# Third layer's first two blocks: corners weighted and summed inside the attention instead of after it, with the second layer's remaining work spread anew

## The chip, the cores and the metric

The kernel runs on one core of one Trainium2 chip. A core has TensorE (PE, matrix multiplies), VectorE (DVE), ScalarE (ACT), GpSimd (POOL), SyncE (SP, which issues DMAs), and 16 DMA engines. Each engine works through its own queue of instructions in order. The metric is the device time of one execution in microseconds (us), as the median of several runs.

## The reference, cut to what matters

Four layers follow each other on an image batch x of shape (2, 256, 64, 64), all in float32.

- Layer 0: a group norm, then self-attention with 4 heads of 64 channels over the 4096 pixels of each image, a projection, and a residual.
- Layer 1: a position term is added.
- Layer 2 (the "second layer" of the code): a bottleneck. A 1x1 convolution to 64 channels, a modulated deformable 3x3 convolution, a 1x1 convolution back to 256 channels, and a residual.
- Layer 3 (the "third layer"): group norm, ReLU, deformable 3x3 convolution, and that once more, with a residual.

A deformable convolution samples the image, for each pixel and each of nine taps, at a computed place between pixels. The sample is a weighted sum of four corners:

```python
out = gather(y0, x0) * (wy0 * wx0) + gather(y0, x0 + 1) * (wy0 * wx1) \
    + gather(y0 + 1, x0) * (wy1 * wx0) + gather(y0 + 1, x0 + 1) * (wy1 * wx1)
off = conv(conv(x, dw, groups=C), pw)          # where to sample
res = einsum('bckhw,ock->bohw', sampled, w)    # nine taps, 256 channels in, 256 out
```

## The kernel before

**Two phases.** `attention` holds layer 0 and 1 and, in the gaps, most of layer 2 and the very beginning of layer 3. `deform` holds the rest of layer 2 and layer 3. The order of instructions on PE, ACT, DVE and POOL is the order in which the Python program emits them.

**Attention.** The loop variable n runs over 1024 tiles of scores (4 units of 256; a block is 16 tiles) and advances by 2, so an *iteration* is two tiles. For each tile PE makes scores (L580), DVE takes their maximum (L592), ACT takes exponentials (L598), PE transposes them (`turn`, L610), DVE and ACT copy the transposes out of PSUM (`keep`, L627 and L629), and PE multiplies them with the values (`attend`, L639). Exponentials are emitted one iteration ahead of their transposes. Once per block, POOL scales the block's output with shares that SP has written to DRAM and loaded back (`spread`, L506 and L510; `combine`, L519, L520, L525).

**Early samples.** In the last unit `early_samples` computes sampling places for the first two blocks (EARLY = 2) of 512 pixels of layer 3, image 0. Two blocks of 9 taps by 4 groups of 128 pixels are 72 *steps*. For each, the inner function `gather` lets POOL fetch all four corners of 128 pixels (128 rows of 4 KB, L846), and SP stores this raw tile into the DRAM tensor `samp_d` (L1259). `self.sample()` calls it once at the end of each iteration, and twice where n % 16 is 10, 12 or 14.

**Deform.** The loop variable s runs over 1152 steps (4 passes of 8 blocks of 36 steps). `gather(s + 8)` fetches corners (POOL, L846; for the first 72 steps a load from `samp_d`, L1445). `first` multiplies the first corner by its weight on ACT (L1459). `others` adds the other three on DVE, one scalar_tensor_tensor each (L1465). `turn` transposes the sample on PE (L1477), `evacuate` copies it out on ACT (L1486), and `product` multiplies it with the convolution's weights on PE (L1496).

**Side work.** A `Side` emits pieces of another computation between the steps. `second` is the deformable convolution of layer 2 for image 1: 144 conv steps, each with two gathers on POOL (`bfour`, L846), a multiplication (L1065) and two additions (L1075, L1076) on DVE, kept eight tiles deep. It advances by up to 0.9 s + 2.5 min(s, 72) pieces, two pieces a conv step. When it is through, `image` of pass 1 is started, 0.9 pieces a step; whatever is left of it is emitted at s = 228. `offs` holds the sampling places of the next blocks (its matmuls are L803 and L823).

```python
seconds = Side(0, 0.9, second, lambda s: 2.5 * min(s, EARLY * BLOCK))
...
images.append(Side(s, 0.9, image(*layers[1])))
```

Of the kernel before, what the change touches and what calls it, by code (L numbers as in the profile page):

```python
# [64 lines left out]
class Net:  # L65
    def __init__(self, ctx, tc, a, out):
        self.tc, self.nc, self.a, self.out = tc, tc.nc, a, out
        nc = self.nc
        const = ctx.enter_context(tc.tile_pool(name="const", bufs=1))
        self.small = ctx.enter_context(tc.tile_pool(name="small", bufs=2))  # L70
        dram = ctx.enter_context(tc.tile_pool(name="dram", bufs=1, space=DRAM))

        self.ident = const.tile([P, P], F32, name="ident")
        make_identity(nc, self.ident)
        self.vec = const.tile([P, V_COLS], F32, name="vec")
        nc.sync.dma_start(self.vec, a["vec"])
        self.sel = const.tile([P, 32], F32, name="sel")
        self.shift = const.tile([P, DWK, 32], F32, name="shift")
        self.later = [(self.sel, a["sel"]), (self.shift, a["shift"])]

        self.img2, self.img3, self.x2d = [], [], []

        self.xn_d, self.xa_d = [], []
        for b in range(B):
            self.img2.append(dram.tile([GH * GW, 2 * CM], F32, name=f"img2_{b}"))
            self.img3.append(dram.tile([GH * GW, 2 * C], F32, name=f"img3_{b}"))
            self.x2d.append(dram.tile([C, HW], F32, name=f"x2d_{b}"))
            self.xn_d.append(dram.tile([C, HW], F32, name=f"xn_{b}"))
            self.xa_d.append(dram.tile([C, HW], F32, name=f"xa_{b}"))

        self.pos_d = dram.tile([C, HW], F32, name="pos_d")

        self.samp_d = [dram.tile([4 * K2 * P, 4 * C], F32, name=f"samp_d{i}") for i in range(EARLY)]
        self.sample = lambda: False
        self.early = {}
        self.share_d = [dram.tile([16, P], F32, name=f"share_d{n}") for n in range(2)]

        vec = self.vec
        self.bn_s = const.tile([P, 4], F32, name="bn_s")
        self.bn_t = const.tile([P, 4], F32, name="bn_t")  # L100
        rstd = self.rsqrt(vec[:, V_BNV : V_BNV + 4], 4)
        nc.vector.tensor_mul(self.bn_s, rstd, vec[:, V_BNG : V_BNG + 4])
        m = self.small.tile([P, 4], F32, name="bn_m")
        nc.vector.tensor_copy(m, vec[:, V_BNM : V_BNM + 4])

        nc.vector.tensor_sub(m[:, 1:2], m[:, 1:2], vec[:, V_DCNB : V_DCNB + 1])
        nc.vector.tensor_mul(m, m, self.bn_s)
        nc.vector.tensor_sub(self.bn_t, vec[:, V_BNB : V_BNB + 4], m)

        for v in (self.bn_s, self.bn_t):  # L110
            nc.vector.tensor_copy(v[CM:P, 0:2], v[0:CM, 0:2])
# [69 lines left out]
    def attention(self, bott):  # L181
# [5 lines left out]
        with ExitStack() as ctx:  # L187
# [489 lines left out]
            while n < last + 4 or back or more or any(own.values()):  # L677
                u, d = divmod(n, per_unit)
                if d == 0 and u < len(units):
                    plan_unit(u)  # L680
                    if u == 0:
                        back.append(prepare(1))
                    if u == 1:
                        back.append(bott.before(0, bt, ps))
                    if u == 2:
                        back.append(first_batch())
                    if u == 3:
                        back.insert(0, bott.before(1, bt, ps))
                        back.append(self.early_samples(bott, bt, held, xp, vp, kp, ps))

                def small(at):
                    steps = own.pop(at, ())
                    for f in steps:
                        f()
                    if not steps and u > 1:
                        background(1)

                if n - 1 in pts:
                    p = pts.pop(n - 1)
                    keep(n - 1, p, "ACT")  # L700
                    keep(n - 1, p, "DVE")
                ps.flush()
                sc = [scores(m) for m in (n + 2, n + 3) if m < last]
                for m in range(len(sc)):
                    lowest(n + 2 + m, sc[m])
                if n < last:
                    p = turn(e.pop(n))
                    keep(n, p, "DVE")
                if sc:
                    e[n + 2] = exponentials(n + 2, sc[0])  # L710
                if n < last:
                    keep(n, p, "ACT")

                small(n)
                if 4 <= n < last + 4:
                    attend(n - 4)
                    attend(n - 3)
                small(n + 1)
                if n < last:
                    pts[n + 1] = turn(e.pop(n + 1))  # L720
                if sc:
                    e[n + 3] = exponentials(n + 3, sc[1])
                if u or n % 8 == 0:
                    background(1)

                for _ in range(1 + (n % 16 in (10, 12, 14))):
                    more = self.sample()
                n += 2
# [486 lines left out]
    def early_samples(self, bott, pools, held, xp, vp, kp, ps):  # L1215
# [33 lines left out]
            self.filters(wf[cb], cb, dw, pw)  # L1249
            yield True  # L1250
        free = deque(x.rearrange("p u n -> p (u n)") for x in xbs)
        gathers, stores = deque(), deque()

        def gather():


            if len(stores) > 1 and len(free) < 3 or not gathers and stores:
                dst, four = stores.popleft()
                nc.sync.dma_start(dst, four)  # L1259
                free.append(four)  # L1260
            if gathers:
                dst, idx = gathers.popleft()
                four = free.popleft()
                self.gather(four, self.img3[0], idx)
                stores.append((dst, four))
            return gathers or stores

        self.sample = gather
        for i in range(EARLY):
            idx = bott.corner.tile([P, 4, K2], I32, name="bidx")  # L1270
            w4 = self.early[i] = bott.corner.tile([P, 4, K2, 4], F32, name="bw4")
            steps = self.offsets(
                i, xs,
                lambda s, row: wf[s][:, DWK * row : DWK * row + DWK, :].rearrange(
# [19 lines left out]
                free.extend(whole)  # L1294
            for m in range(4 * K2):
                k, j = divmod(m, 4)
                gathers.append((self.samp_d[i][m * P : m * P + P, :], idx[:, j, k : k + 1]))

    def deform(self, bott):

# [4 lines left out]
        with ExitStack() as ctx:  # L1305
# [90 lines left out]
                        yield  # L1396

            IMAGE = 4 + 6 * NB + 1
            corners = {(0, 0, i): (None, w4) for i, w4 in self.early.items()}

            def offsets(b, l):
                if b == 0:
# [20 lines left out]
            layers = [(b, l) for l in range(2) for b in range(B)]  # L1423
            BLOCK = 4 * K2
            LAYER, ALL = NB * BLOCK, len(layers) * NB * BLOCK
            AHEAD, LEAD = 8, BLOCK + 16
            due = {}
            fours, smps, pts, sts, outs, ress = {}, {}, {}, {}, {}, {}

# [3 lines left out]
                return n, i, r // 4, r % 4  # L1433

            def gather(s):
                if s < ALL:
                    n, i, k, j = parts(s)
                    b, l = layers[n]
                    fours[s] = gp.tile([P, 4, C], F32, name="four")
                    four = fours[s].rearrange("p s c -> p (s c)")  # L1440
                    if n == 0 and i < EARLY:

                        queue = nc.gpsimd if s < AHEAD else nc.sync
                        m = 4 * k + j
                        queue.dma_start(four, self.samp_d[i][m * P : m * P + P, :])  # L1445
                        return
                    idx = corners[b, l, i][0]
                    self.gather(four, self.img3[b], idx[:, j, k : k + 1])

            def weight(s, c):  # L1450
                n, i, k, j = parts(s)
# [2 lines left out]

            def first(s):

                if s < ALL:
                    smps[s] = sp.tile([P, C], F32, name="smp")
                    nc.scalar.mul(smps[s], fours[s][:, 0], weight(s, 0))  # L1459

            def others(s):
                if s < ALL:
                    four = fours.pop(s)
                    for c in range(1, 4):
                        nc.vector.scalar_tensor_tensor(  # L1465
# [86 lines left out]
            OFFS = 24  # L1552
            inner = ExitStack()
            second = bott.conv(1, bott.pools(inner, 8), ps)
            for s in range(AHEAD):
                gather(s)
                conv_weight(0, s)
            conv_weight(0, AHEAD)
            begun = offsets(0, 0)
            next(begun)  # L1560
            load(0, self.xn_d[0], wp)
            offs = [Side(EARLY * BLOCK - LEAD - 6, OFFS / BLOCK, begun)]
            first(0)


            last = Side(0, 1, bott.last(1, bott.kept, ps))
            seconds = Side(0, 0.9, second, lambda s: 2.5 * min(s, EARLY * BLOCK))
            stats[0] = self.norm_stats()
            images = []
            for s in range(ALL + 12):  # L1570
                n = s // LAYER
                if s == LAYER:
                    stats[1] = self.norm_stats()
                gather(s + AHEAD)
                first(s + 1)
                others(s)
                if (s - 6) % 4 == 0:
                    evacuate((s - 6) // 4)
                product(*divmod(s - 7, 4), s)
                turn(s - 2)  # L1580
                for f in due.pop(s, ()):
                    f()
                last.follow(s)
# [120 lines left out]
```

## Time and profile before

| what | us |
|---|---|
| runs (3) | 5145.72, 5151.03, 5154.88; median 5151.03 |
| span of the profiled execution (the page has no other time for it) | 5149.0 |
| attention, from the span's start to its last products | about 2980 |
| deform, first 72 steps (transposes of step 0 to step 72) | 2997.6 to 3335.2 |
| transposes of step 158 / 228 | 3548.1 / 3664.8 |
| PE / DVE / ACT / POOL busy over the span | 4816.8 / 4196.7 / 2883.6 / 2254.7 |

The page cuts the span into 40 slices of 128.7 us; each digit is the busy share of an engine in tenths. A group line names the line, the engine, the operation and the tiles, then the count, the busy time, the mean in ns, and the idle time before these instructions with what ended it. A window line gives busy times of PE, PE weight loads, DVE, ACT and POOL, then the granted PE clock, the DMA share and GB/s.

### The profile page before, as it was taken

How to read it: one execution, taken by the hardware profiler on the slowest of the kernel's cores; microseconds unless marked ns; L12 is line 12 of the kernel's file. 1: busy time of each engine (PE TensorE's matmuls, PEld its weight loads, DVE VectorE, ACT ScalarE, POOL GpSimd, SP SyncE). 2: the span in 40 equal slices, each digit the busy share in tenths (PEclk: the TensorE clock that was granted, in tenths of full speed). 3: DMA queues.
4: the chain of work that ended last, by engine and by line, in shares of the span. 5: the costliest groups of instructions: out<-in, count | busy, mean ns of one | idle time of the engine just before them, and what ended most of it. 6: DMA issues, size and time to landing. Idle time of an engine off the chain costs nothing. (4 is left out here: it accounts for less than half of the span.)

```text
span 5149.0 us, 100000 instructions
## 1 busy us (share of the span) xinstructions
PE 4816.8 (94%) x38200; PEld 2651.9 (52%) x38200; DVE 4196.7 (82%) x7929; ACT 2883.6 (56%) x5221; POOL 2254.7 (44%) x2256
## 2 busy tenths in 40 slices
PE   8999999999999999999999957679999999999998
PEld 5555565555565555565555523234444444444443
DVE  6878867878668888687766768878999999999998
ACT  5666656666666666666656622235444554454444
POOL 0111111111107777464023257775666566666665
PEclk9999999999999999999999967789999999999999
DMA  5231121111113333322557677679999999999998
GB/s 172 61 99 51 42 68 49 35 46 30 55 52 94 93 100 102 94 85 79 150 193 272 233 242 239 207 251 376 340 329 339 360 359 350 356 388 346 347 348 318
DMA packets 367022, 997.66 MB, mean 194 GB/s; under 512 B 61372, under 2 KB 98810, under 8 KB 366542
## 3 DMA queue, kind: packets, MB, share of 16 engines
q0 software_dynamic: 196560, 690.41, 37.7%
q1 hardware_dynamic: 169438, 300.73, 17.9%
q8 instruction: 300, 4.92, 0.4%
q14 instruction: 180, 1.47, 0.1%
q10 hardware_dynamic: 544, 0.13, 0.0%
HBM read 855.36 MB, written 127.35 MB: 191 GB/s over the span
## 5 line engine op out<-in xcount | busy, mean ns | idle before, releaser
L1465 DVE SCALAR_TENSOR_TENSOR smp<-four,dw,smp 128x256 f32<-128x256 f32 x3240 | 1503.8, 483 | 122.3 <-ACT smp L1459 44.4
L598 ACT ACTIVATE e<-sc,low 128x1024 f32<-128x1024 f32 x1024 | 1147.1, 1120 | 745.1 <-DVE low L592 741.4
L592 DVE TENSOR_REDUCE low<-sc 128x1 f32<-128x1024 f32 x1024 | 1204.8, 1218 | 228.1 <-PE sc L580 224.0
L846 POOL DMA_INDIRECT four<-img,didx x1080 | 1085.4, 1005 | 646.3 <-DVE smp L1465 349.2
L1496 PE MATMUL out<-st,wc 128*128 128x512 f32 x2304 | 1229.6, 616 | 65.0 <-ACT st L1486 33.6
L580 PE MATMUL sc<-k,qs 64*128 64x512 f32 x2048 | 997.1, 605 | 1.8 <-ACT e L598 1.4
L639 PE MATMUL av<-et,v 128*64 128x256 f32 x8192 | 996.5, 385 | 0.0
L580 PE MATMUL sc<-k,q 64*128 64x512 f32 x2048 | 977.3, 604 | 0.0
L519 POOL TENSOR_TENSOR o<-o,f 128x1024 f32<-128x1024 f32 x63 | 149.3, 2370 | 1771.5 <-DMA f<-share_d 890.1
L610 PEld LDWEIGHTS tt<-ident,e 64*128 64x128 f32 x16384 | 651.7, 139 | 519.3 <-issue 275.4
L1459 ACT ACTIVATE smp<-four,dw 128x256 f32<-128x256 f32 x1080 | 535.9, 507 | 594.3 <-PE pt L1477 460.4
L610 PE MATMUL tt<-ident,e 64*128 64x64 f32 x16384 | 726.1, 226 | 40.5 <-ACT et L629 19.9
L629 ACT COPY et<-tt 128x512 f32<-128x512 f32 x1152 | 659.5, 586 | 170.5 <-PE tt L610 169.2
L627 DVE COPY et<-tt 128x512 f32<-128x512 f32 x896 | 612.0, 683 | 161.3 <-PE tt L610 160.9
L639 PEld LDWEIGHTS av<-et,v 128*64 128x64 f32 x8192 | 552.1, 137 | 302.9 <-issue 48.4
L1477 PEld LDWEIGHTS pt<-ident,smp 128*128 128x128 f32 x2304 | 320.5, 144 | 740.8 <-issue 423.4
L846 POOL DMA_INDIRECT bfour<-img,bidx x576 | 581.0, 1009 | 184.2 <-issue 90.3
L1496 PEld LDWEIGHTS out<-st,wc 128*128 128x128 f32 x2304 | 392.0, 196 | 323.3 <-issue 216.5
L1477 PE MATMUL pt<-ident,smp 128*128 128x128 f32 x2304 | 454.6, 280 | 72.7 <-DVE smp L1465 67.1
L580 PEld LDWEIGHTS sc<-k,qs 64*128 64x128 f32 x2048 | 345.4, 188 | 215.7 <-issue 120.0
L1486 ACT COPY st<-pt 128x1024 f32<-128x1024 f32 x288 | 291.2, 1011 | 289.5 <-PE pt L1477 287.8
L803 PE MATMUL pd<-x,wf 128*126 128x512 f32 x840 | 433.4, 598 | 0.0
(183 smaller groups left out, 3600.4 us busy)
## 6 DMA issues: line engine op xcount, KB each, us to landing
f<-share_d SPq DMA_DIRECT2D x128, 256.0 KB
four<-samp_d SPq DMA_DIRECT2D x64, 512.0 KB
xb<-xn SPq DMA_DIRECT2D x55, 512.0 KB
img<-imgt SPq DMA_DIRECT2D x96, 256.0 KB
four<-img,didx POOLq DMA_INDIRECT x1080, 6.1
xa<-res SPq DMA_DIRECT2D x32, 512.0 KB
samp_d<-xb SPq DMA_DIRECT2D x32, 512.0 KB
xb<-in_x SPq DMA_DIRECT2D x20, 512.0 KB
```

The costliest lines, as they stand in the source:

```text
L580: nc.tensor.matmul(s[:, j, :], lhsT=q[u, i // 2][int(h != j)][halves[j], at : at + P], rhs=k[u][c][halves[j], h, :], start=True, stop=True,)
L592: nc.vector.tensor_reduce(low, s, AX.X, ALU.max, negate=True)
L598: nc.scalar.activation(e.rearrange("p j n -> p (j n)"), s, AF.Exp, bias=blk.low[:, g, c : c + 1], accum_out=blk.sum[:, g, c : c + 1],)
L610: nc.tensor.transpose(pt[:, m, :], e[half, m // 4, m % 4 * P : m % 4 * P + P], self.ident[half, half],)
L627: nc.vector.tensor_copy(dst, pt)
L629: nc.scalar.copy(dst, pt)
L639: nc.tensor.matmul(now["av"][halves[h], :], lhsT=v[u][c][:, m, halves[h]], rhs=ets[j][:, m, h, :], start=(m == 0), stop=(m == 7),)
L846: self.nc.gpsimd.indirect_dma_start(out=dst, out_offset=None, in_=img, in_offset=bass.IndirectOffsetOnAxis(ap=idx, axis=0),)
L1459: nc.scalar.mul(smps[s], fours[s][:, 0], weight(s, 0))
L1465: nc.vector.scalar_tensor_tensor(smps[s], four[:, c], weight(s, c), smps[s], ALU.mult, ALU.add)
L1477: nc.tensor.transpose(pts[u][:, c, j * P : (j + 1) * P], smp[:, c * P : c * P + P], self.ident,)
L1496: nc.tensor.matmul(outs[ob], lhsT=wc[k][:, c, ob * P : ob * P + P], rhs=sts[u][:, c, :], start=(k == 0 and c == 0), stop=(k == K2 - 1 and ...
```

## The change

In the attention, the inner `gather` no longer stores raw corners. It keeps four lists. A call may (a) store a finished sum that was entered at least three counts ago, now 128 KB instead of 512 KB; (b) multiply the first corner of a tile gathered at least two counts ago by its weight, on ACT; (c) gather into a free buffer. A new function `sums`, called once in each iteration right after a `keep`, takes up to two scaled tiles: even ones get three scalar_tensor_tensor on DVE, odd ones a multiplication of 768 and additions of 512 and 256 elements per partition on POOL. Each sum advances the count too.

In deform, the first 72 steps have no `gather`, `first` or `others`. `kept` loads four steps' sums in one DMA, 16 steps ahead, for the first 16 steps on POOL's queue and then on SP's; `turn` transposes straight from the loaded tile. Only four of these loads stand among the nine weight loads ahead of the loop, where eight loads stood. `kept` and `gather` move behind `turn` in the loop. `second` gets 8 pieces at once, none more up to s = 32, and then 2.15 a step.

```diff
-        self.samp_d = [dram.tile([4 * K2 * P, 4 * C], F32, name=f"samp_d{i}") for i in range(EARLY)]
+        self.samp_d = [dram.tile([4 * K2 * P, C], F32, name=f"samp_d{i}") for i in range(EARLY)]
...
                     keep(n, p, "DVE")
+                self.sums()
                 if sc:
                     e[n + 2] = exponentials(n + 2, sc[0])
...
         def gather():
-            if len(stores) > 1 and len(free) < 3 or not gathers and stores:
-                dst, four = stores.popleft()
-                nc.sync.dma_start(dst, four)
-                free.append(four)
-            if gathers:
-                dst, idx = gathers.popleft()
-                four = free.popleft()
-                self.gather(four, self.img3[0], idx)
-                stores.append((dst, four))
-            return gathers or stores
+            now = next(calls)
+            if stores and stores[0][0] <= now - 3:
+                _, dst, four = stores.popleft()
+                nc.sync.dma_start(dst, four[:, :C])
+                free.append(four)
+            if raw and raw[0][0] <= now - 2:
+                _, item, four = raw.popleft()
+                nc.scalar.mul(four[:, :C], four[:, :C], item[2][:, 0:1])
+                scaled.append((item, four))
+            if gathers and free:
+                item, four = gathers.popleft(), free.popleft()
+                self.gather(four, self.img3[0], item[1])
+                raw.append((now, item, four))
+            return gathers or raw or scaled or stores
+
+        def sums():
+            for _ in range(min(2, len(scaled))):
+                (dst, _, w, m), flat = scaled.popleft()
+                four = flat.rearrange("p (s c) -> p s c", c=C)
+                if m % 2:
+                    nc.gpsimd.tensor_mul(
+                        four[:, 1:4], four[:, 1:4],
+                        w[:, 1:4].unsqueeze(2).to_broadcast([P, 3, C]),
+                    )
+                    nc.gpsimd.tensor_add(four[:, 0:2], four[:, 0:2], four[:, 2:4])
+                    nc.gpsimd.tensor_add(four[:, 0], four[:, 0], four[:, 1])
+                else:
+                    for c in range(1, 4):
+                        nc.vector.scalar_tensor_tensor(
+                            four[:, 0], four[:, c], w[:, c : c + 1], four[:, 0],
+                            ALU.mult, ALU.add,
+                        )
+                stores.append((next(calls), dst, flat))
...
-            AHEAD, LEAD = 8, BLOCK + 16
+            AHEAD, LEAD, KEPT, SOON = 8, BLOCK + 16, EARLY * BLOCK, 16
...
-                    if n == 0 and i < EARLY:
-                        queue = nc.gpsimd if s < AHEAD else nc.sync
-                        m = 4 * k + j
-                        queue.dma_start(four, self.samp_d[i][m * P : m * P + P, :])
-                        return
...
+            def kept(s):
+                if s < KEPT and s % 4 == 0:
+                    _, i, k, _ = parts(s)
+                    t = gp.tile([P, 4, C], F32, name="four")
+                    src = self.samp_d[i].rearrange("(k j p) c -> k p j c", j=4, p=P)
+                    queue = nc.gpsimd if s < SOON else nc.sync
+                    queue.dma_start(t, src[k])
+                    for j in range(4):
+                        smps[s + j] = t[:, j]
...
-                if s < ALL:
+                if KEPT <= s < ALL:
                     smps[s] = sp.tile([P, C], F32, name="smp")
...
-            for s in range(AHEAD):
-                gather(s)
-                conv_weight(0, s)
-            conv_weight(0, AHEAD)
+            for k in range(K2):
+                if k < SOON // 4:
+                    kept(4 * k)
+                conv_weight(0, k)
...
-            seconds = Side(0, 0.9, second, lambda s: 2.5 * min(s, EARLY * BLOCK))
+            QUIET, QUICK = 32, 2.15
+            seconds = Side(
+                0, 0, second, lambda s: 8 + QUICK * max(0, s - QUIET)
+            )
...
-                gather(s + AHEAD)
                 first(s + 1)
                 others(s)
...
                 turn(s - 2)
+                kept(s + SOON)
+                gather(s + AHEAD)
```

More of the change, by code (lines that the diff above doesn't have):

```diff
@@ L91, in __init__ @@
         self.pos_d = dram.tile([C, HW], F32, name="pos_d")
-        self.samp_d = [dram.tile([4 * K2 * P, 4 * C], F32, name=f"samp_d{i}") for i in range(EARLY)]
+        self.samp_d = [dram.tile([4 * K2 * P, C], F32, name=f"samp_d{i}") for i in range(EARLY)]
         self.sample = lambda: False
-        self.early = {}
+        self.sums = lambda: None
         self.share_d = [dram.tile([16, P], F32, name=f"share_d{n}") for n in range(2)]
@@ L1251, in early_samples @@
         free = deque(x.rearrange("p u n -> p (u n)") for x in xbs)
-        gathers, stores = deque(), deque()
+        gathers, raw, scaled, stores = deque(), deque(), deque(), deque()
+        calls = itertools.count()
         def gather():
-            if len(stores) > 1 and len(free) < 3 or not gathers and stores:
-                dst, four = stores.popleft()
-                nc.sync.dma_start(dst, four)
+            now = next(calls)
+            if stores and stores[0][0] <= now - 3:
+                _, dst, four = stores.popleft()
+                nc.sync.dma_start(dst, four[:, :C])
                 free.append(four)
-            if gathers:
-                dst, idx = gathers.popleft()
-                four = free.popleft()
-                self.gather(four, self.img3[0], idx)
-                stores.append((dst, four))
-            return gathers or stores
+            if raw and raw[0][0] <= now - 2:
[25 more added lines that the diff above has]
+                stores.append((next(calls), dst, flat))
+        self.sums = sums
         self.sample = gather
@@ L1270, in early_samples @@
             idx = bott.corner.tile([P, 4, K2], I32, name="bidx")
-            w4 = self.early[i] = bott.corner.tile([P, 4, K2, 4], F32, name="bw4")
+            w4 = bott.corner.tile([P, 4, K2, 4], F32, name="bw4")
             steps = self.offsets(
@@ L1296, in early_samples @@
                 k, j = divmod(m, 4)
-                gathers.append((self.samp_d[i][m * P : m * P + P, :], idx[:, j, k : k + 1]))
+                dst = self.samp_d[i][m * P : m * P + P, :]
+                gathers.append((dst, idx[:, j, k : k + 1], w4[:, j, k], m))
     def deform(self, bott):
@@ L1398, in deform @@
             IMAGE = 4 + 6 * NB + 1
-            corners = {(0, 0, i): (None, w4) for i, w4 in self.early.items()}
+            corners = {}
             def offsets(b, l):
@@ L1455, in first @@
             def first(s):
-                if s < ALL:
+                if KEPT <= s < ALL:
                     smps[s] = sp.tile([P, C], F32, name="smp")
@@ L1461, in others @@
             def others(s):
-                if s < ALL:
+                if KEPT <= s < ALL:
                     four = fours.pop(s)
@@ L1562, in deform @@
             offs = [Side(EARLY * BLOCK - LEAD - 6, OFFS / BLOCK, begun)]
-            first(0)
             last = Side(0, 1, bott.last(1, bott.kept, ps))
-            seconds = Side(0, 0.9, second, lambda s: 2.5 * min(s, EARLY * BLOCK))
+            QUIET, QUICK = 32, 2.15
+            seconds = Side(
+                0, 0, second, lambda s: 8 + QUICK * max(0, s - QUIET)
+            )
             stats[0] = self.norm_stats()
```

## The prediction, made before the changed kernel was run

> **What bounds the kernel now.** I read the slices first, for where PE is not full:
>
> ```profile
> PE   8999999999999999999999957679999999999998
> DVE  6878867878668888687766768878999999999998
> POOL 0111111111107777464023257775666566666665
> ```
>
> PE is full except in slices 23 to 26, about 2960 to 3475 us: the front of deform, where the second layer for image 1 stands between the first steps of layer 3. The windows tell its limit (columns: PE, PE loads, DVE, ACT, POOL, PE clock):
>
> ```profile
> 2750.00:2850.00 100.00, 94.32 (x990) 55.73 (x987) 67.11 (x106) 64.95 (x121) 29.37 (x28) 0.98 0.76 278
> 3015.00:3025.00 10.00, 0.36 (x2) 0.29 (x2) 4.47 (x11) 0.00 (x0) 5.07 (x5) 0.50 0.63 221
> 3100.00:3150.00 50.00, 37.50 (x113) 16.80 (x112) 44.03 (x98) 13.81 (x25) 38.52 (x38) 0.82 0.74 244
> 3350.00:3400.00 50.00, 31.85 (x92) 15.83 (x88) 36.18 (x89) 14.41 (x25) 38.72 (x38) 0.76 0.71 230
> 4000.00:4500.00 500.00, 478.02 (x1736) 232.57 (x1735) 473.32 (x1118) 250.47 (x432) 311.90 (x311) 1.00 0.97 357
> ```
>
> DVE varies between 36 and 44 of 50 us; POOL stands at 38.5 to 38.7 with 38 gathers whatever DVE does. Its timeline shows why 77% is full:
>
> ```profile
> 3368.23 0.94 POOL L846 DMA_INDIRECT four<-img,didx  x1 [0.30 <-ACT smp L1459]
> 3369.48 1.07 POOL L846 DMA_INDIRECT four<-img,didx  x1 [0.30 <-issue]
> 3370.85 1.00 POOL L846 DMA_INDIRECT bfour<-img,bidx  x1 [0.30 <-issue]
> ```
>
> Each gather is followed by 0.30 us, whoever is named. So **POOL's gathers, not DVE, set the front**: 288 of the second layer and 48 of layer 3 from 3004.2 to 3459.4, 455.2/335 = 1.36 us each (50/38 = 1.32 in undisturbed windows). Behind it (last window) PE and DVE are both full. The cost of the added work is read in the attention's sampling stretch, 2613 to 2926; from the waits and groups there:
>
> ```profile
> POOL o L519 <- DMA f<-share_d: 90.4, 4, 25.3
> DVE o L471 <- POOL avs L525: 16.5, 4, 6.2
> L598 ACT ACTIVATE e<-sc,low 128x1024 f32<-128x1024 f32 x113 | 126.6, 1120 | 78.2 <-DVE low L592 77.9
> L519 POOL TENSOR_TENSOR o<-o,f 128x1024 f32<-128x1024 f32 x7 | 16.5, 2353 | 165.4 <-DMA f<-share_d 121.9 <-DVE o L471 23.5 <-DVE et L627 19.9
> L520 POOL TENSOR_TENSOR o<-o 128x512 f32<-128x512 f32 x7 | 8.9, 1270 | 0.6
> L525 POOL TENSOR_TENSOR avs<-o 128x256 f32<-128x256 f32 x7 | 5.1, 726 | 0.5
> ```
>
> An iteration takes 5.03 to 5.9 us, PE nearly full, ACT and DVE with a little air.
>
> **The front, step by step.** *Removed:* 216 scalar_tensor_tensor:
>
> ```profile
> L1465 DVE SCALAR_TENSOR_TENSOR smp<-four,bw,smp 128x256 f32<-128x256 f32 x216 | 104.4, 484 | 10.0 <-ACT smp L1459 4.9
> L846 POOL DMA_INDIRECT bfour<-img,bidx x288 | 296.9, 1031 | 98.9 <-issue 48.5 <-DVE smp L1465 11.6 <-DVE bfour L1065 8.5
> ```
>
> 104.4 us of DVE and 34 of ACT go, but no gather goes with them. The gain is what POOL gains.
>
> *Start.* Before, 8 loads of 512 KB, 9 of 256 KB and 4 of 1 MB went out before the second layer's first gathers, and SP added raw loads; the DMA engines moved 400 GB/s, and the first of those tiles landed at 3020. Now 8.7 MB stand ahead: 22 us from 2977, so I let POOL gather from 3000.
>
> *The hold.* Up to s = 32 the second layer has only 8 pieces (16 gathers). But DVE and POOL do not wait for PE's step number: they run ahead to the first DVE instruction that needs a late PE result, the corner places of the next block, about s = 46. That lets 14 conv steps through, 28 gathers; 44 gathers at 1.345 last to 3059. PE's steps need about 1.5 us: 2987 + 46 x 1.5 = 3056, 3060 with a cold start. So POOL hardly pauses; I allow 5 us. Here a row and a rule part: the granted clock is 0.50 at 3015 and 0.76 to 0.82 later. Did PE stay at 0.5, a step would cost 3 us, step 46 come at 3125, and POOL lose 65 us. The Trainium skill (TensorE: Matmul & The Clock Gate, "What's actually happening") has the clock go full after about 3.4 us of sustained work; the 4000:4500 window, 96% busy at 1.00, agrees, and the low rows are those with an idle PE. I take the rule.
>
> *How many gathers.* The last gather of the second layer is piece 7 + 2 x 136 = 279. 8 + 2.15 (s - 32) = 279 gives s = 158; by then layer 3 has gathered for steps 72 to 166, 95 tiles. 288 + 95 = 383, at 1.345 (between 1.32 and 1.36): 3000 + 515 + 5 = **3520**. Before, this point was s = 111, and PE stood at 116, so PE's steps lead POOL's by some 6: step 164 at 3520, against 3560 before (transposes by their times). **-40**.
>
> *Given back.* The rest of the second layer, 5 steps at about 2.9 us, ends at step 169 (3534), not 131. Only then starts `image`, 51 pieces at 0.9: 57 steps, to 226, just inside 228. Steps with it took (3603.6 - 3499.0)/57 = 1.835 us, plain ones 1.57. So step 228 comes at 3534 + 105 + 3 = 3642, against 3664.8: **-23**. Behind it the code is as before.
>
> *Moved loads.* Eighteen loads by fours in runs of 1 KB, 4 on POOL's queue (0.57 us each instead of 8) and 14 on SP's (0.32 each, 64 before). No row has their landing; a 512 KB load in 4 KB runs lands in 8.1. They go out 16 steps ahead, 24 us or more, so even 16 us is hidden behind the steps; uncovered it costs 8 once. Moving `kept` and `gather` behind `turn` changes no engine's own order: nothing.
>
> **The attention, step by step.** *ACT* gets 72 multiplications at 0.507 (L1459): 36.5 us, against 78 us in which it waits for DVE before exponentials. Behind one in ACT's queue stand the copies of PE's transposes; their air is about 0.4 us in every other iteration. Where two fall into one iteration I charge 0.3: 22 x 0.3 = **+6**.
>
> *DVE* gets 36 x 3 x 0.483 = 52 us; behind them stand the copies and the next maxima. Its idle before a maximum differs:
>
> ```profile
> 2716.79 2.35 DVE L592 TENSOR_REDUCE low<-sc 128x1 f32<-128x1024 f32 x2 [1.83 <-PE sc L580]
> 2721.57 2.36 DVE L592 TENSOR_REDUCE low<-sc 128x1 f32<-128x1024 f32 x2 [0.20 <-PE sc L580]
> ```
>
> 1.45 fits into the first; in the second sort (0.7 in pieces) it pushes by 0.75, of which PE feels about 0.4: 18 x 0.4 = **+7**. A check: between 1600 and 2000 DVE was 84% busy, as it would be here, and PE still 98%.
>
> *POOL* gets 36 sums. No row has 768 elements; between 1270 (512) and 2353 (1024) it is 1.8, so 1.8 + 1.27 + 0.73 = 3.8 us, 137 in all. With gathers and `combine` a block of 8 iterations costs 11 x 1.25 + 5.5 x 3.9 + 4.5 = 40 us of its 40 to 47. Tight, not over.
>
> *Shared port.* The Trainium skill (SBUF — State Buffer, "Who interferes with whom") speaks against splitting this between DVE and POOL: a DVE instruction with two SBUF inputs and a POOL one that reads SBUF exclude each other for a whole instruction. The trace agrees in kind: the second layer's multiplication (L1065) takes 0.686 beside gathers and 0.914 where POOL adds in the attention. If each DVE sum waited out a whole POOL sum it would be 36 x 3.8 = 137 us; by the row 108 x 0.23 = 25 us on DVE, mostly into its air. I take the row, **+3** for PE (0 to 40).
>
> *Waits.* ACT waits for its gather, one iteration (5.0 to 5.75 us) later in its order; a lone gather lands in 4.3 us (issued at 2646.7, the store that waits for it leaves at 2651.0), a second one close behind it in about 6.4. By the order POOL starts an odd sum as soon as ACT's product is there, and the gathers behind it still land in time. I take 0, and 0 to 70 for the range. SP's stores waited for gathers in bursts, which made `f` late, held POOL (90.4) and then DVE (16.5); PE was idle 11 of 313 us. Stores of sums wait less: **-10** (0 to -11). By the counts in the code the first gather falls into iteration 902 as before, the last store into 1018 (before, about 1008): still ahead of the last tile, 1024, so hidden; each iteration beyond would add some 5 us. Sum: 6 + 7 + 3 - 10 = **+6**.
>
> **Sum.** 5149.0 (span) - 23 + 6 = 5132; the runs' median stands 2 above the span: **5134 us**. 0.2% (10 us) is about what a measurement tells from no change.
>
> **Rivals.** *(B) ScalarE waits for gathers, slower.* If POOL, 85% loaded, is 2 us late with its gathers, each of the 58 sampling iterations loses about 1 us: 5134 + 58 = 5192. For it: 4.3 us against 5.0 leaves 0.7, and everything attention does queues behind ACT. Against: half the iterations have no POOL sum. It decides from 17/58 = 0.3 us an iteration on; half again as late gives 5220. *(C) The hold starves POOL.* If DVE cannot run ahead, POOL stops at 16 gathers until s = 33, about 3042: 3042 + 367 x 1.345 = 3536 plus the waits, step 228 at 3662: 5151 - 3 + 6 = 5154. For it: it holds if any DVE instruction behind the held pieces needs PE earlier than I see; against: those of the first steps come with PE still early (step 19 at about 3015). *(D) DVE sets the front.* All 104.4 return: 5151 - 104 + 17 (image) + 6 = 5070. Against: POOL's constant 38 gathers.
>
> **How the numbers follow.** A 0.45 (5110 to 5146 by itself), B 0.33, C 0.15, D 0.05, others 0.02. A gives faster 0.41, same 0.04; B slower 0.31, same 0.02; C same 0.10, slower 0.05; D faster: faster 0.46, same 0.16, slower 0.38. The range 5095 to 5195 leaves out D and B's upper third.
>
> **What would show it.** Right: PE dense at full clock from 3000 to 3060; POOL at 38 gathers per 50 us from 3060 to 3520; the second layer's last gather near 3520; step 228 near 3642; no ACT wait on gathers above a few us. Wrong: ACT waiting for `xb` or `v` gathers in the attention, its end later than 2990, or POOL below 35 gathers per 50 us.

## The result, and the profile after

The changed kernel takes 5202.95 us in the median (4 runs, 5198.75 to 5205.58), the kernel before 5148.38 beside it (4 runs, 5144.68 to 5154.88): 1.0104 of the time before (95% interval 1.009 to 1.0118), **55 us slower**. The forecast was 5134, and its range ended at 5195. The profiled execution of the changed kernel has a span of 5203.8 us.

The slices of the changed kernel's page (40 of 130.1 us; busy tenths):

```profile
PE   8999999999999999999998877667999999999998
DVE  6878767878678888687678846777999999999998
POOL 0111111111117777463046647776566566666665
```

The weak slices of PE now begin at the 22nd, inside the attention (before, at the 24th, with the front), and the front still has its dip. Two marks divide the time: the start of the last maximum (`low`, L592), which ends the attention's DVE work, and the first transpose of step 228.

| mark, from the traces | before | after | predicted move | moved |
|---|---|---|---|---|
| last maximum, us from the start | 2963.9 | 3017.3 | +6 | **+53.4** |
| step 228, us after the last maximum | 700.8 | 702.3 | -23 | **+1.5** |

So the whole loss lies in the attention, and the front gained nothing. A window of the attention and three of the front, changed kernel (columns: PE, PE loads, DVE, ACT, POOL, PE clock, DMA share, GB/s):

```profile
2750.00:2850.00 100.00, 85.44 (x836) 48.83 (x832) 82.88 (x123) 62.06 (x123) 63.77 (x57) 0.91 0.52 165
3085.00:3097.00 12.00, 11.92 (x44) 5.85 (x43) 6.54 (x25) 3.61 (x5) 0.00 (x0) 1.00 0.27 88
3118.00:3128.00 10.00, 10.00 (x36) 5.06 (x35) 0.44 (x2) 1.12 (x2) 0.24 (x1) 1.00 0.25 77
3200.00:3250.00 50.00, 29.55 (x93) 13.47 (x92) 37.07 (x80) 12.98 (x24) 38.42 (x39) 0.76 0.67 217
```

In the attention PE fell from 94 of 100 us to 85, while DVE rose from 67 to 83. In the front POOL stands still twice, for about 12 and 10 us, with PE full beside it, and otherwise makes 39 gathers in 50 us, where it made 38.

Where DVE's time went, by its groups from 2650 to 3015 (count, busy, mean ns, idle before); the last line is the kernel before, from 2650 to 2980:

```profile
L1289 DVE SCALAR_TENSOR_TENSOR xb<-xb,bw 128x256 f32<-128x256 f32 x33 | 24.2, 732 | 0.8
L1289 DVE SCALAR_TENSOR_TENSOR k<-k,bw 128x256 f32<-128x256 f32 x24 | 21.4, 891 | 0.6
L1289 DVE SCALAR_TENSOR_TENSOR v<-v,bw 128x256 f32<-128x256 f32 x27 | 20.5, 758 | 0.7
L1289 DVE SCALAR_TENSOR_TENSOR bx<-bx,bw 128x256 f32<-128x256 f32 x24 | 16.4, 683 | 0.6
L487 DVE TENSOR_TENSOR sum<-sum,w 128x16 f32<-128x16 f32 x7 | 4.2, 598 | 0.0
...
L487 DVE TENSOR_TENSOR sum<-sum,w 128x16 f32<-128x16 f32 x8 | 1.3, 165 | 0.0
```

The same instruction with the same shape took 484 ns in the kernel before (L1465). Here it takes 763 on average over the 108. Even `sum`, 16 elements a partition and nothing to do with the change, rose from 165 to 598. What these have in common is two tensors read from SBUF; the maxima and the copies out of PSUM keep their times (1217 and 681 ns on either side). The mean hides two kinds: 74 of the 108 overlap none of POOL's arithmetic (its sums and `combine`) and take 482 ns, the other 34 overlap some and take 1373. The timelines of DVE and POOL at one place:

```profile
2805.84 0.68 DVE L627 COPY et<-tt 128x512 f32<-128x512 f32 x1
2806.44 3.94 DVE L1289 SCALAR_TENSOR_TENSOR v<-v,bw 128x256 f32<-128x256 f32 x3
...
2811.55 2.35 DVE L592 TENSOR_REDUCE low<-sc 128x1 f32<-128x1024 f32 x2
```

```profile
2807.20 1.47 POOL L1281 TENSOR_TENSOR bx<-bx,bw 128x768 f32<-128x768 f32 x1
2808.75 1.34 POOL L1285 TENSOR_TENSOR bx<-bx 128x512 f32<-128x512 f32 x1
2810.17 0.79 POOL L1286 TENSOR_TENSOR bx<-bx 128x256 f32<-128x256 f32 x1
```

Three instructions that need 1.45 us take 3.94. The three of POOL lie beside them, and the next maxima, for which ACT's exponentials wait, come some 2.5 us later for it.

The waits of the changed kernel (us in total, times, longest): ACT's two lines from 2613 to 3010, then PE's, POOL's and DVE's in the front up to 3130.

```profile
ACT e L598 <- DVE low L592: 105.8, 55, 4.9
ACT xb L1266 <- DMA xb<-img,bidx: 1.6, 1, 1.6
...
PE pm L1032 <- ACT bod L1019: 21.7, 1, 21.7
POOL bfour L847 <- DVE bsmp L1077: 23.4, 5, 12.6
POOL bfour L847 <- DMA img<-imgt: 12.1, 1, 12.1
DVE bsmp L1077 <- PE pm L1087: 19.7, 1, 19.7
```

ACT hardly waits for gathers (1.8 us with the group `v`): rival B did not happen. It waits for maxima, 105.8 us here against 82.2 from 2613 to 2960 before. The last four lines are about the front and are read in the section on why the prediction was wrong.

### The profile page after: what moved, and what is told of

Same layout as the page of the kernel before. It is cut to its first block, busy times and chain, and to the rows that moved or that the text cites. A ratio compares the mean times of both kernels' runs of the same rounds, so it can differ in the third digit from the quotient of the medians.

```text
span 5203.8 us, 99837 instructions
## 1 busy us (share of the span) xinstructions
PE 4835.3 (93%) x38200; PEld 2659.3 (51%) x38200; DVE 4191.2 (81%) x7821; ACT 2878.9 (55%) x5221; POOL 2369.0 (46%) x2360
## 3 DMA queue, kind: packets, MB, share of 16 engines
q14 instruction: 180, 1.47, 0.1%
## 4 chain that ended last, share of the span: by engine, by line
PE 34%; DVE 16%; issue 5%; DMA 4%; ACT 2%; POOL 2%; SPq 0%; DVEq 0%; ACTq 0%; POOLq 0%
PE out L1530 11%; DVE smp L1499 8%; PE pd L804 6%; PE av L639 4%; PE sc L580 4%; DMA bfour<-img,bidx 3%; PE pt L1511 3%; PE tt L610 3%; DVE low L592 2%; POOL bfour L847 1%; DVE et L627 1%; DVE bfour L1066 1%; ACT e L598 1%; PE pd L824 1%; ACT st L1520 1%
## 5 line engine op out<-in xcount | busy, mean ns | idle before, releaser
L592 DVE TENSOR_REDUCE low<-sc 128x1 f32<-128x1024 f32 x1024 | 1205.0, 1218 | 213.8 <-PE sc L580 208.8
L1530 PE MATMUL out<-st,wc 128*128 128x512 f32 x2304 | 1233.2, 618 | 129.5 <-ACT st L1520 99.5
L1511 PEld LDWEIGHTS pt<-ident,smp 128*128 128x128 f32 x2160 | 300.6, 144 | 682.5 <-issue 404.8
L1511 PE MATMUL pt<-ident,smp 128*128 128x128 f32 x2160 | 427.2, 280 | 54.1 <-DVE smp L1499 48.7
```

The source lines that it names most:

```text
L592: nc.vector.tensor_reduce(low, s, AX.X, ALU.max, negate=True)
L1511: nc.tensor.transpose(pts[u][:, c, j * P : (j + 1) * P], smp[:, c * P : c * P + P], self.ident,)
L1530: nc.tensor.matmul(outs[ob], lhsT=wc[k][:, c, ob * P : ob * P + P], rhs=sts[u][:, c, :], start=(k == 0 and c == 0), stop=(k == K2 - 1 and ...
```

## The experiments

The runs came in five groups, each on another chip by the record, and each with the kernel before beside it. In one group the kernel before took 5153 us, about as above; in the other four it took 5310 to 5343. The last section shows where that time lies; its cause is open. Ratios are therefore to the kernel before of the same group. In the expectations, the port theory (P) says that VectorE's two-input instructions are shut out while GpSimd reads SBUF. Its rivals put the attention's loss on VectorE's added load (L), on GpSimd's added time (G), or on ScalarE's waits for gathers (A).

**Fills in place of GpSimd's sums.** POOL is as long busy, but only writes.

```diff
                 if m % 2:
-                    nc.gpsimd.tensor_mul(...); nc.gpsimd.tensor_add(...); nc.gpsimd.tensor_add(...)
+                    for c0, c1 in ((1, 4), (1, 4), (0, 2), (1, 4), (0, 2)):
+                        nc.gpsimd.memset(four[:, c0:c1], 0.0)
```

> The changed kernel, but each of GpSimd's 36 sums (a multiplication and two additions, 1.48 + 1.29 + 0.74 us) is replaced by five fills of nothing but zeros into the same tile, about as long (3.5 us); the odd samples are left out of the computation. GpSimd stays as busy, but no longer reads SBUF. Theory P (VectorE's instructions with two SBUF inputs are shut out while GpSimd reads SBUF): the scalar_tensor_tensor in the attention go back from 0.68 to 0.89 us to about 0.49, the attention from +53 us to +10 to +18 against before, the time to about 5163. Theory L (VectorE simply has too much work of its own, 52 us more): nothing changes, 5203. Theory G (GpSimd is too busy, its gathers and combine come late): nothing changes, 5203.

Measured 5335.23 us, 0.9985 (0.9971 to 0.9999). The run was repeated beside the changed kernel:

> The changed kernel again, as the measure for the runs beside it, because the last eight ran on a chip where the kernel before takes 5342 us instead of 5148. On a chip like the first: 1.0104 of before, last maximum of the attention at about 3017. On the slower chip: 1.005 to 1.012.

> GpSimd's sums replaced by fills as long, again, beside the changed kernel on the same chip. Theory P: attention 35 to 45 us shorter than the changed kernel's, time 0.7 to 0.9% below it. Theory L or G: no difference over 0.2%. On a chip like the first the maxima's stretch from tile 896 to the last takes about 400 us (before 387, changed 439).

The changed kernel took 5339.95 there, 1.006 (1.0039 to 1.0081), the fills 5298.18, 0.9983 (0.9974 to 0.9992): 42 us less. The last maximum moved from 3030.9 to 2991.8, and VectorE's sums from 772 ns to 502. The instructions of VectorE and the time of GpSimd are nearly unchanged, so L and G alone cannot give this. The ratio under 1 does not say that the rest was free, because in these groups the attention of the kernel before is itself longer than with fills, as the next runs show.

**GpSimd's sums left out; VectorE's sums left out; both.**

```diff
-                    nc.gpsimd.tensor_mul(...)   # and both additions: nopool, nosums
+                    pass
...
-                    for c in range(1, 4): nc.vector.scalar_tensor_tensor(...)   # nodve, nosums
+                    pass
```

> The changed kernel with GpSimd's 36 sums left out (the odd samples are left with the first corner alone). Theory P: as with the fills, +10 to +18 us in the attention, about 5160. Theory L: VectorE still has its 52 us, so +53 stays, 5203. Theory G: GpSimd has room again, +10 or less, about 5155. With the fills this tells P from G.

> The changed kernel with VectorE's 36 sums left out (the even samples keep the first corner alone), GpSimd's kept. Theory P: only VectorE's small two-input instructions still meet GpSimd, +8 to +18 in the attention, about 5162. Theory L: attention as before, about 5150. Theory G: +53 stays, 5203.

> The changed kernel with all 72 sums left out (every sample is the weighted first corner), so ScalarE's 72 multiplications, the gathers and the 128 KB stores remain. What is left over shows the rest of the change: the deform part alone. Theories P, L, G: attention within 5 us of before, time 5145 to 5155 as deform alone was worth about +1 us. Theory A (ScalarE's multiplications and their waits for gathers hold the attention): +15 or more in the attention, 5165 or more.

Measured 1.0036 (1.0025 to 1.0048), 0.9977 (0.9967 to 0.9987) and 1.0023 (1.0006 to 1.0041). Without any sums the last maximum stands at 3010.0, where runs with the attention of the kernel before have 3009.5 to 3018.3 in such groups, so ScalarE's multiplications cost nothing that shows there, which rules A out; what is over in the time lies behind the attention. The first two again, beside the changed kernel at 1.006:

> GpSimd's sums left out, again. Theory P and theory G: 35 to 45 us below the changed kernel, stretch of about 400 us. Theory L: no difference over 0.2%. On the slow chip this run was 0.5% slower than the one with fills; if that is the chip alone, both are within 0.2% here.

> VectorE's sums left out, GpSimd's kept, again. Theory P: 35 to 45 us below the changed kernel, stretch of about 400 us. Theory L: 50 us below, stretch of about 387. Theory G: no difference.

Measured 5323.35, 1.0024 (1.0015 to 1.0034), and 5290.86, 0.996 (0.9946 to 0.9975): 17 and 49 us less than the changed kernel. Without GpSimd's sums VectorE's went down to 510 ns, as the port has it. But the time fell by 17 us only, less than with fills, and that is a miss. The last maxima have a pattern. Where gathers follow each other on GpSimd with nothing between (without its sums, without any, and in the attention of the kernel before), they stand at 3009.5 to 3018.3 in these groups; where fills stand between, or sums without VectorE's beside them, they stand at 2991.8 to 2999.5. In the group at 5153 us it is the other way (2963.2 before, 2973.9 with fills), so a cost of bursts of gathers is possible in the slower groups alone, and its cause is not shown. Without VectorE's sums its remaining instructions still lasted 22 us longer in sum than before; in the changed kernel all of them together lasted 42 longer.

**All sums on VectorE.**

```diff
-                if m % 2:
+                if False:
```

> The changed kernel with all 72 sums on VectorE, none on GpSimd: 216 scalar_tensor_tensor, 104 us of VectorE's own work instead of 52. Theory P: they take 0.484 each, except beside combine; VectorE saves the 30 us of lockout on them and some 12 on its small instructions and gets 52 of work: the attention is +50 to +65 against before, time about 5205. Theory L: cost in step with VectorE's own work, twice 53, time about 5255. Theory G: about 5160.

Measured 5387.64, 1.0083 (1.0056 to 1.0109). The sums are short (520 ns; all of VectorE's instructions together exceed the kernel before by 6 us), yet the last maximum stands at 3049.8. The next run, of the same group and with the changed kernel's attention, has 3042.0. So the port can be avoided in this way, but 52 us more of VectorE's own work cost the attention at least as much as the port did: it has no room for twice the sums.

**The hold removed.**

```diff
-            QUIET, QUICK = 32, 2.15
+            QUIET, QUICK = 0, 2.15
```

> The changed kernel without the quiet first 32 steps: the second layer's pieces start at once, 8 + 2.15 a step, so that they end at about step 137 and not 169. Theory POOL (the gathers set the front, the hold only leaves GpSimd idle for 22 us): the second layer's gathers run through without a pause of over 5 us, last gather 20 to 40 us earlier, time 5175 to 5185. Theory DVE (VectorE sets the front and the hold is what makes use of its freed time): no faster than the changed kernel, 5200 to 5215.

Measured 5344.2, 0.9998 (0.9986 to 1.001). Step 228 came 778.3 us after the last maximum; with the hold it came at 805.5 in the run above, of the same group, and at 801.2 in the changed kernel of another. It is the expected gain of this stage, though GpSimd still paused for up to 14 us, where no pause over 5 was expected.

**VectorE's sums left out of the front, in the kernel before.**

```diff
-                    for c in range(1, 4):
+                    for c in range(1, 4 if s >= EARLY * BLOCK else 1):
```

> The kernel before with VectorE's three additions of the first 72 steps left out (these samples are the weighted first corner alone): 104 us of VectorE's work taken from the front, all else as before. Theory POOL: 336 gathers at 1.28 to 1.30 us instead of 1.36 because fewer two-input instructions of VectorE meet them, 20 to 27 us, time 5121 to 5130. Theory DVE: most of the 104 us, time 5045 to 5070.

Measured 5343.86, 1.0002 (0.9989 to 1.0016). 104 us of VectorE's work bought nothing, and the gain that my own theory expected did not come either. As a test between the two it is weak: in this group GpSimd did not gather without pause, as it does in the profile of the kernel before, but waited 69 us in the front for tiles to come free (5 in that profile). Rival D falls by the runs at 5153 us below: with all of the 104 us gone from the front it is 22.9 us shorter (g_memq0), with half of them 18.8 (h_half).

**The third layer's image loaded after step 4, in the kernel before.**

```diff
-            load(0, self.xn_d[0], wp)
...
+                if s == 4:
+                    load(0, self.xn_d[0], wp)
```

> The kernel before with the 4 MB load of the image for the sampling places (four loads of 1 MB on GpSimd's queue) moved from ahead of the loop to step 4, behind the second layer's first gathers. If the front starts late because these loads stand ahead of the first gathers: the first tile of the second layer lands at about 3010 instead of 3020 and the time is 6 to 12 us less, about 5140. If the start is held by something else, or the later load holds the sampling places up: within 3 us of 5148.

Measured 5339.64, 0.9999 (0.9987 to 1.0011): no gain, a miss. The first gather of the front came only 2 us sooner than in the run above (38.0 against 40.2 us behind the last maximum).

**Both causes at once, and half of the change.** This group was run where the kernel before takes 5153 us.

```diff
# memq0: the fills of above, and
-            QUIET, QUICK = 32, 2.15
+            QUIET, QUICK = 0, 2.15
# half: also with QUIET = 0; even samples are stored raw and weighted in deform, as before
-                nc.scalar.mul(four[:, :C], four[:, :C], item[2][:, 0:1])
+                if item[3] % 2:
+                    nc.scalar.mul(four[:, :C], four[:, :C], item[2][:, 0:1])
...
-                else:
-                    for c in range(1, 4): nc.vector.scalar_tensor_tensor(...)
```

> The kernel before, unchanged, for the stages of its time on this chip. All theories: a ratio of 1 within 0.2%. If the attention of the runs with before's attention holds here, its last maximum comes within 10 us of theirs (3009 to 3014 where before takes about 5310 to 5340; 2964 where it takes about 5150).

> The changed kernel, unchanged, beside the other runs of this call. Its ratio was 1.0104 on one chip and 1.006 on another. If the share of the loss that the attention has is a matter of the shared port alone, the three-operand sums of VectorE take 760 to 775 ns on either chip, and the last maximum comes 20 to 55 us later than in the kernel before.

> Leaves out GpSimd's 36 sums, with fills as long in their place, so those samples are not weighted, and gives the second layer no hold. Theory (port and hold are the two losses and add up): the attention ends 39 to 55 us earlier than in the changed kernel and the front is 22 to 27 us shorter, so 60 to 80 us less than the changed kernel, 0.985 to 0.995 of the kernel before. Rival (the front is held by the landing of gathers, so that an earlier start only waits longer): 40 us less, about 0.998.

> Whole computation kept. Only the odd samples are weighted in the attention, on ScalarE and GpSimd; the even ones are stored raw and weighted behind the attention as in the kernel before, and the second layer is not held. Port theory: without VectorE's 108 sums the attention costs no more than in the run that left these out (on that chip 17 us less than the kernel before, and its smaller two-input instructions still wait some 22 us), and the front is as without the hold, 780 to 790 us on the slower chip: 0.990 to 0.997 of the kernel before. Rival (a GpSimd that reads SBUF costs the attention as much, whoever else sums): 1.000 to 1.006.

| run | median us | ratio (interval) | last maximum | step 228 after it |
|---|---|---|---|---|
| g_before | 5153.61 | 1.0001 (0.9992 to 1.001) | 2963.2 | 702.4 |
| g_after | 5200.1 | 1.0093 (1.0076 to 1.011) | 3012.8 | 701.5 |
| g_memq0 | 5147.68 | 0.9991 (0.9983 to 1.0) | 2973.9 | 679.5 |
| h_half | 5154.3 | 1.0007 (0.9998 to 1.0016) | 2981.5 | 683.6 |

The window 2650 to 2950 of g_before, of g_after and of g_memq0:

```profile
2650.00:2950.00 300.00, 291.73 (x3142) 174.69 (x3139) 211.72 (x345) 205.78 (x386) 89.72 (x84) 0.99 0.73 263
```

```profile
2650.00:2950.00 300.00, 261.58 (x2666) 151.37 (x2664) 255.71 (x387) 194.05 (x381) 190.96 (x170) 0.95 0.52 164
```

```profile
2650.00:2950.00 300.00, 284.15 (x2989) 166.26 (x2987) 251.65 (x431) 220.07 (x433) 203.22 (x257) 0.99 0.60 189
```

With fills DVE is about as busy (252 against 256), having got through 431 instructions instead of 387; POOL is even busier (203 against 191). Yet PE has 284 us of work instead of 262. Two of g_memq0's groups from 2650 to 2950:

```profile
L1285 DVE SCALAR_TENSOR_TENSOR bx<-bx,bw 128x256 f32<-128x256 f32 x24 | 11.8, 494 | 0.6
L487 DVE TENSOR_TENSOR sum<-sum,w 128x16 f32<-128x16 f32 x7 | 1.2, 166 | 0.0
```

In the profiles the two causes are 38.9 us (3012.8 - 2973.9) and 22.0 us (701.5 - 679.5), 60.9 together, the lower end of what was expected. In the medians they are 52 us, between the theory and its rival. The ratio of 0.9991 lies outside the theory's 0.985 to 0.995 and next to the rival's 0.998; the theory's ratio was also mis-worked, since 60 to 80 us below the changed kernel's 5200 make 0.9936 to 0.9975. What is left of the attention's loss without the reads is 10.7 us (2973.9 - 2963.2).

h_half missed: its front is as expected, 18.8 us shorter than before, but its attention still costs 18.3. Two groups of its DVE from 2650 to 2975 say why:

```profile
L488 DVE TENSOR_TENSOR sum<-sum,w 128x16 f32<-128x16 f32 x7 | 7.9, 1123 | 0.0
L492 DVE TENSOR_TENSOR share<-w,total 128x16 f32<-128x16 f32 x7 | 5.6, 802 | 0.2
```

With no long sums of its own, VectorE is shut out with whatever two-input instruction it has: `sum` takes 1123 ns instead of 165. The excess of all of VectorE's instructions over the kernel before is 26.4 us in the stretch from tile 896 on, 20.9 of it on those with two inputs in SBUF. The rest is on a few with one: an operation on `mask` took 2135 ns on the two occasions when it met GpSimd's arithmetic, and 172 otherwise. The rival that I had named for this run, that reading GpSimd costs the attention whoever else sums, is the better description, within its 1.000 to 1.006.

**The even spread alone.** g_memq0 and h_half have a shorter front without much in common but the spread of the second layer. So the kernel before got only that:

```diff
-            seconds = Side(0, 0.9, second, lambda s: 2.5 * min(s, EARLY * BLOCK))
+            seconds = Side(0, 0, second, lambda s: 8 + 2.15 * s)   # k_even175: 1.75
```

> The kernel before with one edit: the second layer gets 8 + 2.15 s pieces. Whole computation kept; the attention is the kernel before's. If the front's gain is that of the even spread (less of the second layer beside the first steps, more gathers of layer 3 before it ends), step 228 comes 680 to 690 us after the last maximum instead of 702: 0.9965 to 0.998. If it belongs to the work that the change removed from the front, it stays at 700: 1.000 within 0.001.

> The same with 8 + 1.75 s pieces, so the second layer ends near step 155 and its image is just through by step 228. Even spread theory: about 379 gathers at 1.32 us from 40 us on, then some 68 steps at 1.8: step 228 at 660 to 675, 0.993 to 0.9955. If the gain belongs to the removed work: 1.000, and slower where the image is left over at step 228.

Measured 5326.97, **0.9973 (0.9961 to 0.9985)**, and 5335.82, 0.9995 (0.9987 to 1.0004). The first does the whole computation and beats both kernels by its ratio: the spread is worth 11 us by itself, with no work moved into the attention. This was measured in a slower group only. Its stages cannot be compared with the kernel before, which has no profile of that group (step 228 is 773.1 us behind the last maximum). The second missed: its last gather of the second layer came 71 us later (644.0 against 573.3), with 28 more gathers of layer 3 before it. At the 1.32 us counted these make 37 us. Most of the rest is GpSimd waiting for a free tile behind VectorE's last addition of the second layer (L1076), 99.5 us in this front against 63.1 in the other; a gather itself took as long in both (1.03 us).

## Why the prediction was wrong

**Shared port, the step that failed.** It charged "+3 for PE (0 to 40)". It costs 39 us: that much comes back when GpSimd writes instead of reading. I had the Trainium skill's rule (SBUF — State Buffer, "Who interferes with whom": a DVE instruction with two SBUF inputs contends with a GpSimd one that reads SBUF, "not with one that only writes it") and the row that agreed in kind, 0.686 against 0.914 us. The size was taken from the row: 0.23 us on each of 108 instructions. Measured is 0.28 us each (763 - 484), 30 us, so the row was nearly right for the sums. It is a mean of two kinds, too: from 1600 to 2000, 42 of its multiplications meet none of POOL's arithmetic and take 680 ns, and 32 meet some and take 1198. Two things were wrong. The rule speaks of every two-input instruction, and I counted the new ones alone; the small ones of the softmax and of the sampling places bring the excess to 41.9 us. And "mostly into its air" was not argued from the place: each delay stands ahead of the next maxima, and PE got nearly all of it. The check at 1600 to 2000 did not warn, though DVE's share was the same: there 27 instructions lost some 18 us beside POOL's arithmetic in 400 us, here 52 lost some 47 in 439, each against the same instruction away from it. The fills agree with the rule's second half: in g_memq0 the 97 sums that meet no `combine` take 482 ns, and all 108 take 550 on average, against 780 in g_after. The other bound, 137 us, where each DVE sum waits out a whole POOL sum, did not happen, since 74 of the 108 met none.

**ACT, DVE, Waits.** Without the reads the attention moved +10.7; the terms 6 + 7 - 10 gave +3. ACT's waits for gathers were taken as 0 and are 1.8 us. POOL's wait for `f` fell from 90.4 to 9.6 us, as described. A POOL sum takes 3.5 us (1.47 + 1.29 + 0.74), against the 3.8 counted.

**The hold.** "So POOL hardly pauses; I allow 5 us" is the second step that failed: POOL stood still for 12.6 and 9.9 us. That DVE runs ahead to the next PE result was right; where PE then was, was not. Step 46 was put 69 us behind step 0 and came 95.5 behind it (3049.4 to 3144.9). Most of the difference is one wait, PE's 21.7 us on `bod` (L1019), between the transposes of steps 1 and 2; without it a step took 1.60 us, against my 1.5. Behind `bod` stands DVE's first multiplication of the second layer, which waited 24.4 us for the first gather, and that one for the writes of `img`. So PE, ACT, DVE and POOL stopped on one chain at the start. Later DVE stood still for PE, 9.3 us for the matmul of the next places (L1001) and 19.7 us for the transposes of the second layer's samples (L1087), and POOL found no free tile. Without the hold the front is 22 us shorter, and then 23 us below the kernel before. That this is the forecast's figure is luck: it comes with the hold gone and by another path, 352 gathers up to the second layer's last instead of 383. Rival C had the mechanism in part: POOL stopped after 16 gathers, as it said, but for 12.6 us and once more after 32, not until s = 33.

**The other terms of the front.** *Start*: the first gather came 47.6 us behind the last maximum instead of 36.1 (3000 against 2963.9), 11.5 late, 12.1 of it on the writes of `img`. *How many gathers*: 384 instead of 383. The stream took 523.4 us instead of 520; without the two pauses, 500.9, it is 1.30 us each, not 1.345. *Given back*: steps 164 to 169 took 30.5 us, not 14, and the image's 57 steps 100.2, not 105. The former is not the hold's: g_memq0, without it, spends 30.7 us on steps 128 to 133, where its second layer ends. Together, with the pauses in the 3.4, the terms make the missing 24 us: 11.5 + 3.4 + 16.5 - 4.8 = 26.6, less 2.5 by which step 164 was ahead of the last gather. The **clock** rule held: the granted clock was 0.50 from 3040 to 3080, around PE's stop, 1.00 in the windows where PE is full (3085 to 3097, 3118 to 3128), and 0.76 from 3200 to 3250, where PE is 59% busy.

**POOL sets the front.** Partly shown. Removing DVE's work there gained nothing in one slower group, and at 5153 us the front with half of that work left (h_half) is only 4 us longer than with none (g_memq0). But what had the gain is a spread that mixes the two layers' gathers and PE's work more evenly, and that I had not priced by itself.

**The range** would just have held the port's upper bound and a starved POOL together (5134 + 37 + 20 = 5191), both of which were in the text. The measured time lies above it because the front missed by 24 and the other terms of the attention by another 8: 5134 + 36 (port) + 24 + 8 = 5202, against 5203.

## What to carry to other kernels

Before work goes to GpSimd, count every two-input SBUF instruction that VectorE has beside it, old ones too, and ask what stands behind each in VectorE's queue; where that is what the bounding engine waits for, expect the delay to be paid nearly in full: here 39 of 42 us. Change the order of side work and the place of work in separate versions: here the order was worth 11 us in one group, and the move lost 11 to 53 in the attention wherever the kernel before takes 5148 to 5153 us. When a side computation is held back, find the one chain at its start (write, gather, multiply, places) and put every engine's stop on it into the sum.

## What was not expected of the hardware

The kernel before takes 5148 and 5153 us in the median of two groups of runs and 5310 to 5343 in four others, each of these on another chip. The engines' instructions are equally long in both (maxima 1216 to 1218 ns, copies 681). The changed kernel's profile is 132.6 us longer in one of these (c_after, 5336.4 against 5203.8), and 99 of these lie between the last maximum and step 228. What differs are waits, some of which nothing in the trace releases. PE's, from 3000 to 5000 us, of the changed kernel in that group:

```profile
PE out L1530 <- issue: 24.2, 10, 6.4
...
PE pm L1097 <- issue: 19.0, 2, 15.3
```

The same view of the first profile has 0.8 us for the first line and none of the second. The gathers of the front come at some 1.6 us each there, against 1.36, though each takes 1.00 us in both: from the first of them to the second layer's last, GpSimd waits 108 us for free tiles behind VectorE's additions (L1077), against 27. The change costs 1.006 in that group and 1.0093 to 1.0104 otherwise, so a loss measured in such a group cannot be carried over to another unchecked. The cause stays open.
